# Two moves in a turn-by-turn schedule: the next chunk's key products on Pool, and a read-out's second matmul

## The chip, the cores and the metric

The kernel runs on one core of a Trainium2 chip. Its time is the device time of one execution in microseconds, given as the median of several runs. The engines of the core are named as in the profile: PE does matmuls, PEld is PE's loading of weights, DVE is the vector engine, ACT the scalar engine, POOL the GpSimd engine, and SP only issues DMAs here. Each engine, and SP's queue too, takes its instructions strictly in the order in which they were put.

## The reference, cut to what matters

The program is two layers over x of 16 x 512 x 128 in float32. Layer 0 adds two branches that both read xn, the normalized x: a small memory network that is trained chunk by chunk and then read out (the part that the change touches), and a convolution with attention and a dense mixture of 8 experts. Layer 1 is causal attention done twice and a mixture of 32 experts. The branch in question:

```
x  (16 rows, 512 tokens, 128) -> 8 chunks of 64 tokens
k  = rmsnorm(silu(xc @ wk.T), k_norm_w);   v = silu(xc @ wv.T)
def step((mem, surp), chunk):                   # lax.scan over the 8 chunks, in order
    pred  = k_c + rmsnorm(silu(k_c @ w0.T) @ w1.T, ln)
    grads = grad of mean((v_c - pred)**2 * theta_c) in (w0, w1, ln)
    clip  = min(1 / (norm(grads) + 1e-6), 1)
    surp  = eta_c * surp - grads * clip;  mem = beta_c * mem + surp
q  = rmsnorm(silu(x @ wq.T), q_norm_w)
read-out: q + rmsnorm(silu(q @ w0.T) @ w1.T, ln)     # with the last mem
...
x = x + read-out + attention_and_experts(xn)
```

## The kernel before

The whole program is written as Python generators, "stages", that a small loop (class Turns, L277) advances together. In each turn every live stage runs up to its next `yield` and emits its instructions. Stages carry a rank, and the lower rank goes first within a turn: 0 for the maxima of the attention scores (tops, which calls largest), 1 for the weighted sums (back, which calls weighted), 2 for the ends of those, 3 for the scan and the read-outs, 4 for the rest of attention, 6 for the experts (ffn, L547). PE's order is exactly the order of emission. The other engines and the DMA queues are ordered by the framework, which follows the order of emission as far as its own estimate of readiness lets it; what is marked high priority (rsqrt, L209) is put ahead. A wait therefore stops everything behind it on its engine. The number of expert units that ffn emits in a turn depends on what the other stages put on PE in that turn (`load_ns`), so that turns have about equal PE work.

After a start that normalizes x (norm0), layer 0's attention and experts run in every turn from then to about 1480 us, and beside them one stage, scan (L786). It has two parts.

The chunks. step(c) is one step of the scan. It turns the keys k (turned), makes the hidden layer (hidden, whose last two operations run on Pool, L891 and L892), turns it (hidden_turned), and takes the gradient in two halves (gradient, L901). A half begins with the matmul py, an ACT copy to yh (L914), four squares on ACT with their sums, and Pool's rsqrt giving r_y (L213, L214). Three turns later DVE multiplies yh by r_y (L920), and then a row of DVE products follows (L923 to L942), with one Pool product (gy, L935) between. DVE's maxima of the attention scores (nm, L404) stand between them in the same queue, and each pair of score matmuls needs a PSUM bank that such a maximum sets free. One step takes some 41 turns. On Pool, before() also prepares the decayed state (L853 to L857).

The keys of chunk c + 2 are made by project (L817) beside step(c + 1): it is put on the list at the end of step(c). It loads the tokens, makes four halves of k and v (silu_half, L757), squares k on ACT, calls rsqrt for r_k, and then runs three Pool operations of 128 x 1024 elements, one turn apart: k times the gain (L836), k times r_k (L838), and v = k - v (L840). Two turns later it marks ("keys", c), for which step(c) waits at its beginning. ks and the tiles k and v have two buffers.

The read-outs. After the eighth step, readout(b) (L1024) runs for the 16 rows, started six turns apart, so that about four are alive at a time. Counted from its start: the matmul pj with wq in turn 2, squares and Pool's products for q in turn 4, the transposes into qT in turn 9, the two halves of hidden (L1043: matmul ppq, two ACT operations, a DVE product into hTq) in turns 10 and 11, the sixteen-pass matmul pyq with w1 (L1056 to L1059), the ACT copy yq with four squares and r_yq, three turns later a DVE product (L1065) and three Pool operations (L1066 to L1068), and three turns after that the store to acc (L1070). hTq and yq of row b share a buffer with those of row b + 2 (tags "h" and "ds").

Of the kernel before, what the change touches and what calls it, by code (L numbers as in the profile page):

```python
# [73 lines left out]
def bc(ap, axis, n):  # L74

    u = ap.unsqueeze(axis)
    shape = list(u.shape)
    shape[axis] = n
    return u.to_broadcast(shape)
# [3 lines left out]
def network(ctx: ExitStack, tc: tile.TileContext, a, out):  # L83
# [60 lines left out]
    def mark(*m):  # L144
        done[m] = clock[0]
# [17 lines left out]
    def room():  # L163

        while held[0] >= pools["work"]:
            yield

    def hold(name):

        held[0] += 1  # L170
        return work(name)

    def drop():

        read[0] += 1

    def work(name):
        return pools["ps"].tile([P, 512], F32, tag="bank", bufs=7, name=name)

    def toks(ap):  # L180
        return ap.rearrange("p (t d) -> p t d", d=P)

    def flat(ap):
        return ap.rearrange("p t d -> p (t d)")
# [4 lines left out]
    def mm(o, lhsT, rhs, start=True, stop=True):  # L189
        n = int(np.prod(rhs.shape[1:]))  # L190
        if lhsT.dtype == FR:
            load_ns[0] += 0.5 * (0.45 * n + 105)
        else:
            t = 0.42 * n if lhsT.shape[-1] == 32 and n >= P else 2 * max(0.834 * n, 110)
            load_ns[0] += t
            array_ns[0] += t
        nc.tensor.matmul(o, lhsT=lhsT, rhs=rhs, start=start, stop=stop)  # L197
# [59 lines left out]
    def transpose_tokens(dst, src):  # L257

        nc.scalar.copy(dst, turn4(lambda t: src[:, t, :]))

    def rms_rows(dst, y, n, pool):

        ss = sm.tile([P, n], F32, tag="ss", name="ss")
        for t in range(n):
            sq = pool.tile([P, D], F32, tag="junk", name="sq")
            nc.scalar.activation(sq, y[:, t, :], AF.Square, accum_out=ss[:, t : t + 1])  # L266
        rsqrt(dst, ss, 1.0 / D, 1e-6, n)
# [5 lines left out]
    def idle(n):  # L273
        for _ in range(n):
            yield
# [481 lines left out]
    def silu_half(dst, lhs, w):  # L757

        yield from room()
        p = hold("pj")  # L760
        for t in range(4):
            mm(p[:, t * D : (t + 1) * D], lhs(t), w)
        nc.scalar.activation(dst, p, AF.Tanh)
        yield
        nc.vector.scalar_tensor_tensor(dst, dst, 1.0, p, ALU.add, ALU.mult)
        drop()
        yield

    def side(*parts):

        going, parts = [], list(parts)
        while parts or going:
            if parts:
                going.append(parts.pop(0))
            going = [g for g in going if next(g, StopIteration) is not StopIteration]
            yield
# [9 lines left out]
    def scan(s1):  # L786
# [13 lines left out]
        def tokens_of(c):  # L800
            xc = s1.tile([P, B, CHUNK], F32, tag="gy", name="xc")
            nc.sync.dma_start(xc, xt[0].rearrange("b p (c t) -> c p b t", t=CHUNK)[c])
            return xc.rearrange("p b t -> p (b t)")
# [13 lines left out]
        def project(c):  # L817

            xc = tokens_of(c)
            yield from idle(3)  # L820
            k = s1.tile([P, NT, D], F32, tag="k", bufs=2, name="k")
            v = s1.tile([P, NT, D], F32, tag="v", bufs=2, name="v")

            def half(dst, w, q):
                return silu_half(
                    flat(dst[:, 4 * q : 4 * q + 4, :]),
                    lambda t: xc[:, (4 * q + t) * P : (4 * q + t + 1) * P], A(w),
                )

            yield from side(half(k, "wk", 0), half(k, "wk", 1), half(v, "wv", 0), half(v, "wv", 1))  # L830
            ks[c] = k, v
            mark("read", c)
            rk = sm.tile([P, NT], F32, tag="r_k", name="r_k")
            rms_rows(rk, k, NT, s1)
            yield
            nc.gpsimd.tensor_tensor(k, k, bc(row["kn"], 1, NT), ALU.mult)  # L836
            yield
            nc.gpsimd.tensor_tensor(k, k, bc(rk, 2, D), ALU.mult)  # L838
            yield
            nc.gpsimd.tensor_tensor(v, k, v, ALU.subtract)  # L840
            yield from idle(2)
            mark("keys", c)

        def step(c):
# [138 lines left out]
            if c + 2 < NC:  # L983
                turns.stages.append((turns.turn, 3, project(c + 2)))
# [32 lines left out]
            yield  # L1017

        turns.stages.append((turns.turn, 3, project(0)))
        turns.stages.append((turns.turn + 12, 3, project(1)))  # L1020
        for c in range(NC):
            yield from step(c)

        def readout(b):  # L1024
            xb = s1.tile([P, TB, D], F32, tag=("k", "v")[b % 2], bufs=2, name="xb")
            nc.sync.dma_start(xb, x_b[b])
            xT = s1.tile([P, S], F32, tag=("hT0", "kT")[b % 2], name="xTr")
            nc.sync.dma_start(xT, xt[0, b])
            yield from idle(2)
            q = s1.tile([P, TB, D], F32, tag=("yh", "eb", "gy", "hT1")[b % 4], name="rq")  # L1030
            yield from silu_half(flat(q), lambda t: xT[:, t * P : (t + 1) * P], A("wq"))
            rq = sm.tile([P, TB], F32, tag="r_q", name="r_q")
            rms_rows(rq, q, TB, s1)
            nc.gpsimd.tensor_tensor(q, q, bc(row["qn"], 1, TB), ALU.mult)
            nc.gpsimd.tensor_tensor(q, q, bc(rq, 2, D), ALU.mult)
            yield from idle(5)
            yield from room()
            qT = s1.tile([P, S], F32, tag="sg", bufs=2, name="qT")
            transpose_tokens(qT, q)
            yield from idle(1)  # L1040
            hT = s1.tile([P, 2, S], F32, tag=("h", "ds")[b % 2], name="hTq")

            def hidden(i):  # L1043
                yield from room()
                pp = hold("ppq")
                mm(pp, w0T[:, i * P : (i + 1) * P], qT)
                nc.scalar.activation(hT[:, i, :], pp, AF.Tanh, scale=0.5)
                nc.scalar.activation(hT[:, i, :], hT[:, i, :], AF.Copy, scale=0.5, bias=0.5)
                yield
                nc.vector.tensor_tensor(hT[:, i, :], hT[:, i, :], pp, ALU.mult)  # L1050
                drop()
                yield

            yield from side(hidden(0), hidden(1))
            yield from room()
            py = toks(work("pyq"))  # L1056
            for t in range(TB):
                for i in range(2):
                    mm(py[:, t, :], hT[:, i, t * P : (t + 1) * P], w1T[:, i, :], start=(i == 0), stop=(i == 1))  # L1059
            ry = sm.tile([P, TB], F32, tag="r_yq", name="r_yq")  # L1060
            y = s1.tile([P, TB, D], F32, tag=("h", "ds")[b % 2], name="yq")
            nc.scalar.copy(y, py)
            rms_rows(ry, y, TB, s1)
            yield from idle(3)
            nc.vector.tensor_tensor(y, y, bc(ry, 2, D), ALU.mult)  # L1065
            nc.gpsimd.tensor_tensor(y, y, bc(ln, 1, TB), ALU.mult)  # L1066
            nc.gpsimd.tensor_tensor(y, y, q, ALU.add)
            nc.gpsimd.tensor_tensor(y, y, xb, ALU.add)  # L1068
            yield from idle(3)
            nc.sync.dma_start(acc_b[b], y)  # L1070
            yield
# [3 lines left out]
        while live or b < B:  # L1075
            if b < B:
                live.append(readout(b))
                b += 1
            for _ in range(6):
                live = [g for g in live if next(g, StopIteration) is not StopIteration]  # L1080
                yield
# [572 lines left out]
```

## Time and profile before

| what | value |
|---|---|
| time, median of 3 runs (lowest, highest) | 3565.93 us (3565.69, 3568.84) |
| the profiled execution | 3557.66 us, with a span of 3555.9 us from its first to its last instruction |
| mean granted clock of PE | 0.975 |
| scan's steps | from the first memory update at 249.2 us to the eighth at 1132.0 us |
| read-outs | first ppq at 1163.2 us, last store issued at 1475.3 us |
| L836, L838, L840 on Pool | 8 of each; median 2370, 1898 and 2370 ns |
| L920 on DVE | 16, median 686 ns, longest 1561 ns |
| pyq on PE | 256 passes of 275 ns |

Busy time is the union of an engine's instructions. "Idle before" is the time in which an engine had nothing running before an instruction, and the name behind the arrow is what released it. The profiled execution is one run of its own, 8.3 us below the median of the timed runs, so sums are made against it and then carried to the median.

### The profile page before, as it was taken

The numbers are of one execution on the slowest core, as the hardware profiler recorded it, in microseconds if no ns is written. First come the engines' busy times: TensorE is split into PE (matmuls) and PEld (weight loads), VectorE is DVE, ScalarE is ACT, GpSimd is POOL, SyncE is SP. The second block draws the span as 40 slices with busy tenths as digits, with TensorE's granted clock in tenths as the row PEclk, the third lists the DMA queues.
The fourth block names the chain that finished last, engine by engine and source line by source line (L and its number), as shares of the span: only waits on it lengthen the run. The fifth ranks groups of instructions, "written<-read, shape, count | busy, mean of one in ns | idle before, by whom it ended". The sixth has DMA issues, their size and how long they took to land.

```text
span 3555.9 us, 63951 instructions
## 1 busy us (share of the span) xinstructions
PE 3379.7 (95%) x22085; PEld 1897.3 (53%) x22085; DVE 2315.6 (65%) x6045; ACT 2233.4 (63%) x4951; POOL 1508.2 (42%) x2354
## 2 busy tenths in 40 slices
PE   6999999999999999999999999999999999998887
PEld 3445555554555555455555565555555555554443
DVE  5676666656766566556467667666666666567875
ACT  1566766775766787666656666665666666664444
POOL 5323432432431455432544344443444344433654
PEclk7999999999999999999999999999999999998998
DMA  5222222222122332443434443444344443433343
GB/s 178 70 71 77 71 82 74 74 77 83 56 85 86 102 109 87 133 122 102 135 108 122 124 125 115 130 126 121 107 122 122 124 125 98 134 106 98 93 102 93
DMA packets 289794, 370.37 MB, mean 104 GB/s; under 512 B 45984, under 2 KB 141376, under 8 KB 289088
## 3 DMA queue, kind: packets, MB, share of 16 engines
q1 hardware_dynamic: 282304, 359.46, 35.0%
q0 software_dynamic: 7168, 6.82, 1.2%
q8 instruction: 177, 2.90, 0.3%
q14 instruction: 145, 1.19, 0.1%
HBM read 236.58 MB, written 132.99 MB: 104 GB/s over the span
## 4 chain that ended last, share of the span: by engine, by line
PE 50%; DVE 5%; DMA 3%; ACT 1%; POOL 1%; issue 1%; SPq 1%; POOLq 0%; DVEq 0%; ACTq 0%
PE s L197 13%; PE pye L611 10%; PE phe L197 10%; PE pc L197 9%; PE pq L197 1%; DVE s L396 1%; PE fill L206 1%; DVE nm L404 1%; PE tpc L252 1%; PE tp L252 1%; DVE s L403 1%; PE po L197 1%; ACT e L476 1%; DMA rq<-lo 1%; PE pv L197 1%
## 5 line engine op out<-in xcount | busy, mean ns | idle before, releaser
L476 ACT ACTIVATE e<-s 128x512 f32<-128x512 f32 (+1 forms) x2432 | 1278.3, 577 | 556.4 <-PE s L197 517.2
L404 DVE TENSOR_REDUCE nm<-s 128x1 f32<-128x512 f32 (+2 forms) x1408 | 907.5, 682 | 510.1 <-PE s L197 509.2
L396 DVE CUSTOM_DVE_ANT_0 s<-s,sb_const 128x512 f32<-128x512 f32 (+1 forms) x1024 | 623.4, 643 | 390.3 <-PE s L197 388.9
L484 POOL TENSOR_SCALAR_AFFINE_SELECT e<-e 128x128 f32<-128x128 f32 (+2 forms) x1270 | 429.6, 347 | 751.0 <-ACT e L476 726.5
L197 PE MATMUL s<-kx,qx 64*128 64x512 f32 (+3 forms) x3072 | 620.4, 429 | 26.8 <-DMA kx<-rk 13.5
L197 PE MATMUL pc<-e,vp 128*32 128x512 f32 (+3 forms) x6144 | 621.7, 502 | 13.9 <-POOL e L484 7.8
L611 PEld LDWEIGHTS pye<-ew,hTe 128*128 128x128 f32 x4096 | 519.0, 192 | 178.7 <-issue 157.9
L197 PEld LDWEIGHTS s<-kx,qx 64*128 64x128 f32 x3072 | 271.2, 187 | 555.2 <-issue 219.4
L611 PE MATMUL pye<-ew,hTe 128*128 128x128 f32 x4096 | 562.3, 281 | 1.5 <-ACT hTe L601 1.4
L197 PE MATMUL s<-qx,kx 64*128 64x512 f32 (+3 forms) x3072 | 535.7, 356 | 27.2 <-DVE nm L404 8.4
L197 PE MATMUL phe<-x1T,ew 128*128 128x512 f32 x1024 | 551.1, 623 | 7.8 <-DMA ew<-in_ew 3.1
L601 ACT ACTIVATE hTe<-phe,sb_cols 128x512 f32<-128x512 f32 x512 | 354.1, 692 | 245.2 <-PE phe L197 242.8
L197 PEld LDWEIGHTS s<-qx,kx 64*128 64x128 f32 x3072 | 305.5, 188 | 80.4 <-ACT e L476 19.1
L619 POOL TENSOR_TENSOR ac<-ac,y 128x512 f32<-128x512 f32 x128 | 163.9, 1280 | 425.9 <-ACT y L618 363.9
L403 DVE TENSOR_TENSOR s<-s,sb_const 128x256 f32<-128x256 f32 (+1 forms) x384 | 181.6, 515 | 190.5 <-PE s L197 157.4
L197 PEld LDWEIGHTS pc<-e,vp 128*32 128x32 f32 x6144 | 151.4, 110 | 238.1 <-issue 173.2
L197 PEld LDWEIGHTS phe<-x1T,ew 128*128 128x128 f32 x1024 | 158.8, 193 | 75.0 <-issue 44.1
L618 ACT ACTIVATE y<-pye,pr 128x128 f32<-128x128 f32 x512 | 147.5, 370 | 30.6 <-PE pye L611 26.2
L396 DVE DVE_READ_ACCUMULATOR2_ANT nm<- 128x1 f32 x1024 | 144.1, 141 | 0.0
L213 POOL TENSOR_SCALAR rs_t<-ss 128x4 f32<-128x4 f32 (+1 forms) x56 | 12.0, 215 | 221.5 <-ACT sq L266 220.0
L1470 POOL DMA_INDIRECT acc<-eo,sidx x32 | 52.0, 1624 | 72.2 <-DVE eo L1464 26.3
L213 POOL TENSOR_SCALAR rs_t<-ln_mv 128x4 f32<-128x4 f32 x64 | 12.8, 200 | 162.3 <-DVE ln_mv L223 159.4
(302 smaller groups left out, 3906.4 us busy)
## 6 DMA issues: line engine op xcount, KB each, us to landing
ew<-in_ew SPq DMA_DIRECT2D x256, 256.0 KB
kx<-rk SPq DMA_DIRECT2D x192, 256.0 KB
qx<-rq SPq DMA_DIRECT2D x128, 256.0 KB
rq<-hi SPq DMA_DIRECT2D x64, 256.0 KB
rq<-lo SPq DMA_DIRECT2D x64, 256.0 KB
rk<-hi SPq DMA_DIRECT2D x64, 256.0 KB
rk<-lo SPq DMA_DIRECT2D x64, 256.0 KB
qx<-r SPq DMA_DIRECT2D x64, 256.0 KB
```

What stands on the lines that cost most here:

```text
L197: nc.tensor.matmul(o, lhsT=lhsT, rhs=rhs, start=start, stop=stop)
L252: nc.tensor.transpose(tp[:, t * P : (t + 1) * P], src(t), ident)
L396: newest[0] = nc.vector.tensor_tensor_reduce(out=sv[r][:, 0, :], in0=sv[r][:, 0, :], in1=row["caus"][:, S - n :], scale=1.0, scalar=-BIG, ...
L403: nc.vector.tensor_tensor(dg, dg, bc(row["caus"][:, S - P :], 1, per), ALU.add)
L404: newest[0] = nc.vector.tensor_reduce(nm[:, qt, r, t : t + per], sv[r], AX.X, ALU.max)
L476: nc.scalar.activation(e[:, r, 0 : per * n], s[r], AF.Exp, scale=SCALE)
L484: cleared[0] = nc.gpsimd.affine_select(out=ev[:, r, :, 0:P], in_=ev[:, r, :, 0:P], pattern=[[0, per], [1, P]], compare_op=ALU.is_ge, fill= ...
L601: nc.scalar.activation(hs[i], ph, AF.Relu, bias=col("fb", i))
L611: nc.tensor.matmul(pye[0][:, t, :], lhsT=h[:, t * P : (t + 1) * P], rhs=w2[e][:, f, :], start=(f == 0 and t == 0), stop=(f == 3), skip_gro ...
L618: nc.scalar.mul(y[:, t, :], pye[0][:, t, :], pr[:, t, e : e + 1])
L619: nc.gpsimd.tensor_tensor(ac, ac, y, ALU.add)
L1470: nc.gpsimd.indirect_dma_start(out=acc, out_offset=bass.IndirectOffsetOnAxis(ap=sidx[:, e : e + 1], axis=0), in_=eo[:, i, :], in_offset=No ...
```

## The change

In project, the one `yield` between the rsqrt of the keys and the first long Pool operation becomes nine for the chunks 2 to 7; for chunks 0 and 1 it stays one. L836, L838 and L840, and the mark ("keys", c), are emitted eight turns later. No instruction is added or removed, and project's matmuls, ACT operations and DMAs before this point stay in their turns.

In readout, one turn is put between the hidden halves and the matmul pyq. All that follows in this read-out is emitted one turn later: pyq, yq and its squares, r_yq, L1065 to L1068, and the store to acc.

```
         def project(c):
...
             rms_rows(rk, k, NT, s1)
-            yield
+            yield from idle(9 if c > 1 else 1)
             nc.gpsimd.tensor_tensor(k, k, bc(row["kn"], 1, NT), ALU.mult)
             yield
             nc.gpsimd.tensor_tensor(k, k, bc(rk, 2, D), ALU.mult)
             yield
             nc.gpsimd.tensor_tensor(v, k, v, ALU.subtract)
             yield from idle(2)
             mark("keys", c)
...
         def readout(b):
...
             yield from side(hidden(0), hidden(1))
+            yield from idle(1)
             yield from room()
             py = toks(work("pyq"))
```

`idle(n)` (L273) yields n times.

More of the change, by code (lines that the diff above doesn't have):

```diff
@@ L834, in project @@
             rms_rows(rk, k, NT, s1)
-            yield
+            yield from idle(9 if c > 1 else 1)
             nc.gpsimd.tensor_tensor(k, k, bc(row["kn"], 1, NT), ALU.mult)
@@ L1054, in readout @@
             yield from side(hidden(0), hidden(1))
+            yield from idle(1)
             yield from room()
```

## The prediction

> **What bounds the kernel now.** I read the page's first part, then the busy times by stretch, then the waits of the scan, then the timelines of single engines round one wait.
>
> ```profile
> PE 3379.7 (95%) x22085; PEld 1897.3 (53%) x22085; DVE 2315.6 (65%) x6045; ACT 2233.4 (63%) x4951; POOL 1508.2 (42%) x2354
> ...
> 630.00:760.00 130.00, 126.76 (x750) 71.66 (x751) 86.74 (x162) 88.81 (x201) 47.22 (x46) 0.99 0.25 71
> 760.00:890.00 130.00, 121.56 (x683) 65.99 (x684) 80.44 (x149) 82.19 (x192) 42.20 (x38) 0.96 0.29 88
> 1300.00:1470.00 170.00, 161.43 (x932) 85.13 (x932) 101.89 (x177) 130.84 (x342) 92.52 (x96) 0.97 0.33 100
> ```
>
> PE is the bound, in a fixed order, so only PE's idle time can be won: 130.00 less 126.76 is 3.2 us in one scan step, 8.4 us in the next, and 8.6 us in the second half of the read-outs. Whatever leaves PE waiting anywhere is paid in full, since all later work stands behind it in PE's order.
>
> Next, who waits for Pool. In the waits of 300 to 1160 us (who, for whom, us, times, longest):
>
> ```profile
> DVE yh L920 <- POOL r_y L214: 22.0, 5, 9.9
> PEld s L197 <- DVE nm L404: 31.8, 38, 5.1
> PE s L197 <- DVE nm L404: 13.8, 10, 4.2
> ```
>
> The last two lines are PE waiting for DVE's maxima. The first is DVE standing still for Pool's rsqrt. The timelines of Pool, DVE and PE in step 5 show the link:
>
> ```profile
> 792.88 2.73 POOL L836 TENSOR_TENSOR k<-k,sb_rowsA 128x1024 f32<-128x1024 f32 x1
> 795.55 1.65 POOL L214 TENSOR_TENSOR r_k<-rs_t,nhalf 128x8 f32<-128x8 f32 x1
> 797.28 1.90 POOL L838 TENSOR_TENSOR k<-k,r_k 128x1024 f32<-128x1024 f32 x1
> 799.25 2.34 POOL L840 TENSOR_TENSOR v<-k,v 128x1024 f32<-128x1024 f32 x1
> 801.96 1.01 POOL L214 TENSOR_TENSOR r_y<-rs_t,nhalf 128x4 f32<-128x4 f32 x1
> ...
> 803.00 0.69 DVE L920 TENSOR_TENSOR yh<-yh,r_y 128x512 f32<-128x512 f32 x1 [6.28 <-POOL r_y L214]
> ...
> 804.34 0.79 PE L197 MATMUL s<-kx,qx 64*128 64x512 f32 x2 [4.23 <-DVE nm L404]
> ```
>
> The three key operations stand before r_y of the second gradient half; DVE waits 6.28 us for r_y, the maxima are behind that, and PE stops for 4.23 us.
>
> **Part 1, the keys.** Nothing is added or removed: six times (chunks 2 to 7) 2.37 + 1.90 + 2.37 = 6.64 us of Pool move eight turns. A turn is (1132.0 - 249.2) / 7 / 41 = 3.1 us, so they move 25 us. They start at 270.5, 412.0, 541.1, 651.0, 792.9 and 921.6 us. In the steps of 270.5 and 651.0 they lie well ahead of both halves' r_y; in the other four they lie between the two r_y, and there alone DVE waits at the second half: 9.90, 3.63, 6.28 and 1.18 us.
>
> What goes: without the three, r_y ends 1.4 us after its last square. In the steps of 541, 793 and 922 that is before DVE gets there, so all of the wait goes. In the step of 412 the square ends at 414.25, r_y at 415.6, and DVE has been there since 412.1, so 6.4 of 9.9 go. Sum 6.4 + 3.63 + 6.28 + 1.18 = 17.5 us of DVE. Four DVE products also ran long beside key operations (1561, 1144, 2318 and 1139 ns where 680 is usual), 3.4 us more. Together DVE gets back 20.9 us. PE's gaps put down to DVE's maxima in the 25 us after these four waits are 1.8, 1.7, 4.2 and 3.3 us, 11.0 in all, or 0.53 of PE per us of DVE.
>
> What comes: the three land some 25 us later, at about 295, 437, 566, 676, 818 and 946 us. Pool is idle there (9.3 us before 302.4, 10.8 before 683.0, 10.7 before 447.7, 14.5 before 579.2), so what is queued behind them on Pool is gy (L935), first read by the matmul pln some 20 turns on, an add of the experts, and in one step a layernorm that ends at 830.4 and that PE first reads at 849.7. The mark ("keys") moves to about turn 17 to 21 of a step of 41, still 20 turns ahead of the step that waits for it; were that gone, each turn would cost PE 3.1 us. But here DVE runs the gradient's products, and a product with two SBUF operands that meets a Pool operation is held:
>
> ```profile
> 926.06 1.90 POOL L838 TENSOR_TENSOR k<-k,r_k 128x1024 f32<-128x1024 f32 x1
> ...
> 926.18 2.32 DVE L923 TENSOR_TENSOR gt<-yh,sb_rowsA 128x512 f32<-128x512 f32 x1
> ```
>
> Four of the twelve operations of those steps held a DVE product, by 0.46 to 1.64 us, mean 0.86. Eighteen move (six times three). From below, a third collide as now: 6 x 0.86 = 5.2 us. From above, all at the longest: 18 x 1.64 = 29.5. I take half, since DVE is denser in the gradient than before it but not full: 9 x 0.86 = 7.7 us. Net 20.9 - 7.7 = 13.2 us of DVE, times 0.53: PE gains 7.0 us. Bounds: (20.9 - 5.2) x 0.53 = 8.3 by this ratio and 11.0 if nothing collides; and a loss of (29.5 - 20.9) x 0.53 = 4.6.
>
> The Trainium skill speaks against the move here: "SBUF — State Buffer", section "SBUF: two separate sides", says that a DVE operation with two SBUF inputs and a GpSimd operation take one shared port pair as an exclusive lock for the whole instruction. The pair of rows above agrees: the product started 0.12 us after Pool and ended 0.54 us after it. By the rule alone the worst is every moved Pool operation holding DVE for its whole length, 6 x 6.64 = 39.8 us of DVE, which would turn the gain into an estimated loss of 10 us; the sum above does not use this.
>
> **Part 2, the read-outs.** Sixteen times pyq and all behind it come 3.1 us later. What it can win is one row:
>
> ```profile
> PE pyq L197 <- DVE hTq L1050: 3.0, 1, 3.0
> ```
>
> PE waited for hTq only once, in row 9; elsewhere hTq was ready 1.5 to 6.2 us ahead. So 3.05 us at most, and I take all of it.
>
> Against it, three things. (a) pyq now falls into the turn of the next row's transposes (15 and 9 are equal modulo 6), so ACT has yq's copy and squares ahead of the copy to qT, which ppq needs a turn later. The time from qT's end to ppq is 0.0 to 4.6 us. If qT goes after the copy and one square, as tanh of pj does now, it ends 0.35 us later, and the five rows with less room cost 1.05 us; if after all four squares (0.50 us each), 1.85 us later, 13.2 us over the rows. I take 1.05, the order that the trace shows. (b) The store of row b moves a turn nearer to the first write of hTq of row b + 2. From store to write it is 2.5 us for row 1, where PE then stopped 2.02 us, and 5.9 us or more for all others; one turn comes off that, so one more stall of 3.1 us; I take it. (c) SP's queue waits at this store:
>
> ```profile
> SPq L1070 <- POOL yq L1068: 91.1, 13, 19.0
> ```
>
> Behind the store stand loads for the read-outs, attention and experts. At 1421.63 us the load of x1T went right behind it and PE waited 1.7 us. If it stays behind, 3.1 us more; if it gets in front, 1.7 less; no row decides, so the middle, +0.7. Sum of part 2: -3.05 + 1.05 + 3.1 + 0.7 = +1.8 us, bounds -4.8 and +19.4. The end of the scan hardly moves: the loop over the read-outs goes in groups of six turns, and one more turn fits into the last.
>
> **Sum.** -7.0 + 1.8 = -5.2 us: the profiled execution from 3557.66 to 3552.5, the median from 3565.93 to 3560.7 (the profiled one ran 8.3 us faster, and I carry the difference over).
>
> **The rivals.**
> (B) The wait goes and nothing collides: all 11.0 us and pyq's 3.05, with (a) alone against it: -13.0, 3552.9. For it: only 39 of the gradient's 128 DVE products met a Pool operation of 0.9 us or more at all, and 11 ran long. Against it: the moved operations arrive among just these products.
> (C) DVE's hold takes the place of its wait: all 18 collide at full price, +4.6 + 1.8 = +6.4, 3572.3. For it, the row at 926; against it, the holds of 0.46 us.
> (D) Slower: SP's queue and the shared buffers. Each store one turn later stops what is behind it (loads) or after it (hTq), at 3.1 us a row. With -7.0, -3.05 and +1.05 on the other side it is slower than the bound from six of sixteen rows on; at seven, -9.0 + 21.7 = +12.7, 3578.6. For it: 104 us of SP's waits at this store in 15 of 16 rows. Against it: only two of these reached PE.
> (E) The move does nothing, because the framework orders Pool by readiness and not by emission: 3566. Against it: the keys run as soon as they are emitted.
>
> **How the numbers follow.** Chances: the forecast 0.45, B 0.28, C 0.10, D 0.14, E 0.03. The forecast's own range is 3555 to 3567, and a third of it lies below 3558.8. What a measurement of this kernel can tell from no change is about 0.2%, 7.1 us. Faster: B and a third of the forecast, 0.42. Slower: D and the edge of C, 0.15. Within: the rest, 0.43. The range goes from 3549, where B gets some of the smaller gaps too, to 3572, where C ends; D lies outside.
>
> **What would show it.** Right: the waits of L920 for r_y fall from 23.5 us to about 5, PE's idle time in the four late steps (4.3, 6.9, 8.3, 5.5 us) falls towards the 1.5 to 2.9 of the others, and long products appear among L931 to L942. Wrong: the idle time stays although L920's waits go (C), ppq waits for qT in many rows (a), or loads land late behind acc<-yq (D).

## The result, and the profile after

| kernel | median of the runs | lowest, highest | runs |
|---|---|---|---|
| before | 3565.52 us | 3559.15, 3568.84 | 6 |
| after | 3578.72 us | 3574.25, 3583.32 | 6 |

The ratio is 1.0035, with a 95% interval of 1.0023 to 1.0047: slower, by about 12.5 us, and outside the forecast's range. The profiled execution took 3577.38 us, its span is 3575.6 us, its mean granted clock 0.971 (0.975 before). The page's busy times, and then the busy times by stretch (length; busy time and instructions of PE, PEld, DVE, ACT and POOL; granted clock of PE; DMA share; GB/s), for the stretches shown of before:

```profile
PE 3396.4 (95%) x22085; PEld 1902.6 (53%) x22085; DVE 2319.8 (65%) x6045; ACT 2230.9 (62%) x4951; POOL 1505.2 (42%) x2354
```

```profile
630.00:760.00 130.00, 125.45 (x739) 71.06 (x735) 83.00 (x155) 86.93 (x197) 48.83 (x49) 0.97 0.25 72
760.00:890.00 130.00, 121.67 (x686) 66.03 (x685) 79.07 (x145) 82.89 (x194) 41.39 (x39) 0.96 0.26 80
1300.00:1470.00 170.00, 160.53 (x900) 82.62 (x900) 99.74 (x178) 125.74 (x348) 92.22 (x97) 0.97 0.31 91
```

PE was busy 16.7 us longer with the same 22085 matmuls, and the span grew by 19.7 us. PE's time falls into idle time, time lost to half clock (half of its busy time under a granted clock of 0.5), and the rest, its own work at full clock:

| | before | after | difference |
|---|---|---|---|
| idle | 176.2 | 179.2 | +3.0 us |
| lost to half clock | 70.6 | 79.6 | +9.0 us |
| own work at full clock | 3309.1 | 3316.8 | +7.7 us |

The second row lies within what executions of one order differ by: e1 below, with the order of before on every queue, lost 80.9 us to half clock in its profile.

By stage, the scan up to its last memory update grew from 1132.0 to 1137.8 us with the same 1.5 to 8.3 us of idle time in every step: only half clock grew (20.7 to 28.1 us). From the first to the last ppq it took 291.0 us and now 294.3. A later stretch in layer 1, between the attention's passes at 2150 and 2263 us of before, grew from 112.4 to 121.9 us: 2.8 us more idle time, 3.3 us of half clock and 3.3 us more of PE's own work. Its rows, cut at whole microseconds near these points, in before and then in after:

```profile
2150.00:2263.00 113.00, 112.15 (x838) 66.41 (x837) 77.52 (x239) 74.88 (x158) 51.72 (x111) 1.00 0.44 129
```

```profile
2163.00:2285.00 122.00, 118.36 (x850) 69.76 (x849) 78.39 (x239) 75.93 (x162) 53.16 (x112) 0.97 0.41 119
```

The read-outs' 3.3 us and this stretch's 9.5 us are 12.8 us, by one profile each, against 13.2 us between the medians; the scan's 5.8 us are half clock.

The waits of 300 to 1160 us hold the forecast's main line unchanged (who, for whom, us, times, longest):

```profile
DVE yh L920 <- POOL r_y L214: 22.0, 5, 9.9
```

This should have fallen to about 5. The timelines of Pool and DVE in step 5 (start, us, engine, line, operation, tiles) show why it did not:

```profile
798.49 2.73 POOL L836 TENSOR_TENSOR k<-k,sb_rowsA 128x1024 f32<-128x1024 f32 x1
...
802.89 1.90 POOL L838 TENSOR_TENSOR k<-k,r_k 128x1024 f32<-128x1024 f32 x1
804.86 2.34 POOL L840 TENSOR_TENSOR v<-k,v 128x1024 f32<-128x1024 f32 x1
...
807.57 1.01 POOL L214 TENSOR_TENSOR r_y<-rs_t,nhalf 128x4 f32<-128x4 f32 x1
...
808.61 0.69 DVE L920 TENSOR_TENSOR yh<-yh,r_y 128x512 f32<-128x512 f32 x1 [6.28 <-POOL r_y L214]
```

The keys' three operations stand before r_y exactly as they did (before, L836 started at 792.88 and L920 had the same 6.28 us). They did not move.

In the read-outs the wait of pyq for hTq is gone, and another has come, of s for hTq. That of ppq for qT is not new: it was 0.9 us in before. The waits of PE and of ACT from 1160 to 1490 us:

```profile
PE s L197 <- DVE hTq L1050: 5.7, 2, 5.2
...
PE ppq L197 <- ACT qT L259: 0.8, 1, 0.8
```

```profile
ACT hTq L1047 <- DMA acc<-yq: 6.2, 2, 5.4
```

ACT waits for a DMA, the store of a read-out, before it writes hTq. The 5.4 us are in row 8. The timelines there:

```profile
1310.91 3.14 POOL L237 TENSOR_SCALAR x<-x,ln_mv,ln_rs 128x128 f32<-128x128 f32 x4
...
1315.48 1.27 POOL L245 TENSOR_TENSOR x<-x,sb_rows 128x512 f32<-128x512 f32 x1
1316.71 1.28 POOL L619 TENSOR_TENSOR ac<-ac,y 128x512 f32<-128x512 f32 x1
1317.94 1.28 POOL L1067 TENSOR_TENSOR yq<-yq,sb_rowsA 128x512 f32<-128x512 f32 x1
...
1320.65 1.27 POOL L1069 TENSOR_TENSOR yq<-yq,xb 128x512 f32<-128x512 f32 x1
...
1321.94 0.37 SPq L1071 DMA_DIRECT2D acc<-yq  x1
...
1324.48 0.60 ACT L1047 ACTIVATE hTq<-ppq 128x512 f32<-128x512 f32 x1 [5.41 <-DMA acc<-yq]
...
1325.97 0.69 DVE L1050 TENSOR_TENSOR hTq<-hTq,ppq 128x512 f32<-128x512 f32 x1 [5.83 <-ACT hTq L1048]
...
1326.72 0.79 PE L197 MATMUL s<-qx,kx 64*128 64x512 f32 x2 [5.17 <-DVE hTq L1050]
1327.44 2.07 PE L611 MATMUL pye<-ew,hTe 128*128 128x128 f32 x8
```

Read it upwards from PE: 5.17 us idle for DVE's product, which waited for ACT, which waited for the store of row 6, because hTq of row 8 lies in the buffer of yq of row 6. The store was late because yq's three Pool operations came after the attention's layernorm (L237 to L245) and an add. In before the three ran ahead of that layernorm and the store was issued at 1307.05. Counted from the first ppq of each kernel (1163.2 and 1169.0 us), the store went from 143.9 to 152.9 us: 9 us later, not one turn. The last line shows what came on top: eight passes of pye took 2.07 us, where a group of eight takes 1.16 us at full clock.

### The profile page after: what moved, and what is told of

Read it like the earlier page. It is cut to its first block, busy times and chain, and to the rows that moved or that the text cites. A ratio compares the mean times of both kernels' runs of the same rounds, so it can differ in the third digit from the quotient of the medians.

```text
span 3575.6 us, 63951 instructions
## 1 busy us (share of the span) xinstructions
PE 3396.4 (95%) x22085; PEld 1902.6 (53%) x22085; DVE 2319.8 (65%) x6045; ACT 2230.9 (62%) x4951; POOL 1505.2 (42%) x2354
## 5 line engine op out<-in xcount | busy, mean ns | idle before, releaser
L197 PE MATMUL s<-qx,kx 64*128 64x512 f32 (+3 forms) x3072 | 544.3, 357 | 43.0 <-DVE nm L404 9.1
L618 ACT ACTIVATE y<-pye,pr 128x128 f32<-128x128 f32 x512 | 147.7, 370 | 34.5 <-PE pye L611 29.8
L396 DVE DVE_READ_ACCUMULATOR2_ANT nm<- 128x1 f32 x1024 | 143.9, 141 | 0.0
L213 POOL TENSOR_SCALAR rs_t<-ln_mv 128x4 f32<-128x4 f32 x64 | 12.8, 200 | 175.3 <-DVE ln_mv L223 172.6
```

The lines of the kernel that those rows point to most:

```text
L396: newest[0] = nc.vector.tensor_tensor_reduce(out=sv[r][:, 0, :], in0=sv[r][:, 0, :], in1=row["caus"][:, S - n :], scale=1.0, scalar=-BIG, ...
L618: nc.scalar.mul(y[:, t, :], pye[0][:, t, :], pr[:, t, e : e + 1])
```

## The experiments

None of the kernels leaves out a part of the reference. Ratios are to the kernel before, measured beside it on the same chip, with 95% intervals:

| experiment | median | ratio | interval |
|---|---|---|---|
| e1, part 1 alone | 3567.98 | 1.0002 | 0.999 to 1.0015 |
| e2, pyq a turn later, experts' turns kept | 3569.66 | 1.0013 | 1.0 to 1.0027 |
| e3, experts' new turns alone | 3564.30 | 0.9993 | 0.998 to 1.0005 |
| e4, only what follows yq's squares a turn later | 3577.24 | 1.0027 | 1.0014 to 1.0041 |
| e5, after, with an own buffer for yq | 3559.23 | 0.999 | 0.9981 to 1.0 |
| e6, e4 with the own buffer | 3548.49 | 0.995 | 0.9937 to 0.9963 |
| e7, before with the own buffer | 3554.47 | 0.9969 | 0.9957 to 0.998 |
| e8, the keys really behind r_y | 3558.74 | 0.9987 | 0.9978 to 0.9995 |
| e9, e6 once more | 3562.51 | 0.996 | 0.9945 to 0.9974 |
| e10, e2 with the own buffer | 3567.06 | 0.9981 | 0.9968 to 0.9995 |
| e11, e9 with the keys of four chunks behind r_y | 3555.60 | 0.9947 | 0.9931 to 0.9962 |
| e12, e9 with the keys behind gy | 3573.47 | 0.9991 | 0.9978 to 1.0004 |

The medians of before in the three groups were 3564.86 (e1 to e4), 3563.46 (e5 to e8) and 3573.73 us (e9 to e12), so the ratios are to be compared, not the medians.

### Part 1 alone (e1)

```
-            yield
+            yield from idle(9 if c > 1 else 1)
```

> Part 1 of the change alone on the kernel before. Theory N (the framework puts Pool's key operations where its own estimate has them ready, whatever the turn of their emission): Pool's order, the key operations at 412, 541, 793 and 922 us and DVE's waits for r_y (9.9, 3.6, 6.3, 1.2 us) stay, ratio 1.000 within 0.002. Rival M (the part moves something and takes a share in the loss): waits of L920 other than these, ratio 1.001 to 1.004. This run also serves as a measure of what two executions of one order differ by in time and granted clock.

No change: 1.0002. The order of the instructions on each of the five queues, with what they wait for, is that of before from the first to the last. The framework put the three operations where its estimate of readiness had them, whatever turn they were emitted in. Part 1 changes nothing in the program's order, and everything that after lost comes from part 2.

### Part 2 taken apart (e2, e3, e4)

Part 2 does three things: pyq comes a turn later, the experts' units (which fill the turns by `load_ns`) fall into other turns, and the tail, all from L1065 to the store, comes a turn later. e2 moves pyq but books its load in the old turn, so that PE's order is before's except for pyq's place; the tail moves with it:

```
+            load_ns[0] += 1760.0
+            array_ns[0] += 1760.0
+            yield from idle(1)
+            load_ns[0] -= 1760.0
+            array_ns[0] -= 1760.0
             yield from room()
             py = toks(work("pyq"))
```

> Part 2 alone, pyq one turn later with all behind it, but its PE load is still booked in the old turn, so that the experts' units keep the turns of the kernel before; PE's order differs in pyq's place alone. Theory P (the loss comes from the experts' units that are planned anew, to the end of the experts in layer 1): ratio 0.999 to 1.001, about 3563 to 3567 us. Rival R (the loss lies in the read-outs: hTq, the squares ahead of qT, the later store): ratio 1.003 to 1.004, about 3578 us.

1.0013: between the ranges of the two theories. Its profile has the stop of row 8 that after has (ACT 6.19 us at hTq, then PE 4.71 us), but 112.4 us in the stretch at 2150 us. e3 leaves pyq in its turn and books its load in the next one:

```
+            load_ns[0] -= 1760.0
+            array_ns[0] -= 1760.0
...
-            yield from idle(3)
+            yield from idle(1)
+            load_ns[0] += 1760.0
+            array_ns[0] += 1760.0
+            yield from idle(2)
```

> The kernel before with pyq in its old turn, but its PE load booked one turn later, so that the experts' units take the turns of the kernel after and no read-out moves. Theory P: ratio 1.003 to 1.004, about 3578 us. Rival R: 0.999 to 1.001.

0.9993, no difference in the time, as rival R had it. Its profile holds two opposite ones: from the first to the last ppq it took 283.4 us (291.0 before), and in the stretch at 2150 us 119.1 us (112.4 before). That stretch took 112.4 to 112.7 us in each of the eleven profiles without the experts' new turns, and 119.1, 121.9 and 122.1 us in the three with them (e3, after, e5): its growth comes from these turns. PE's own work at full clock is 3315.5 us in e3, 3316.8 in after and 3315.7 in e5, the three kernels with the experts' new turns; in the other eleven profiles it lies between 3304 and 3311. The score matmuls with qx as the first operand hold most of the difference (336.0 us in before, 343.6 in e3, 344.4 in after).

e4 moves the tail alone, with PE's order that of before:

```
-            yield from idle(3)
+            yield from idle(4)
             nc.vector.tensor_tensor(y, y, bc(ry, 2, D), ALU.mult)
```

> pyq in its old turn; only what is behind yq's squares (DVE's product, Pool's three, the store) one turn later. PE's order is that of the kernel before. Theory P: ratio 0.999 to 1.001. Rival S (SP's queue stands longer behind the later stores, and hTq behind its buffer): ratio 1.002 to 1.004, with loads landing late behind the store and PE gaps before ppq or pyq of 3 us each.

1.0027: the tail alone is slower. The timelines of SP and ACT in row 8:

```profile
1317.09 0.37 SPq L1070 DMA_DIRECT2D acc<-yq  x1
...
1319.66 0.60 ACT L1047 ACTIVATE hTq<-ppq 128x512 f32<-128x512 f32 x1 [4.29 <-DMA acc<-yq]
```

ACT stands 4.29 us, until 2.6 us after the issue of the store, and PE then has a gap of 3.3 us before ppq, which before has not. A gap of 3.05 us before pyq follows 28 us later, but that one stands in before too. From the first to the last ppq e4 took 298.1 us (291.0 before).

### The shared buffer taken away (e5, e6, e7, e9, e10)

hTq and yq of a row get parts of one tile, and the next row but one no longer writes hTq into what yq is being stored from; SBUF is the same for the rest:

```
+        both = [s1.tile([P, 4 * S], F32, tag=("h", "ds")[i], name="hTyq") for i in range(2)]
...
-            hT = s1.tile([P, 2, S], F32, tag=("h", "ds")[b % 2], name="hTq")
+            hT = both[b % 2][:, 0 : 2 * S].rearrange("p (i s) -> p i s", i=2)
...
-            y = s1.tile([P, TB, D], F32, tag=("h", "ds")[b % 2], name="yq")
+            y = toks(both[b % 2][:, 2 * S : 3 * S])
```

> The kernel after, with yq beside hTq in its buffer and not over it, so that hTq of row b + 2 no longer waits for the store of row b; PE's order is that of the kernel after. Theory B (the loss is ACT standing at hTq for the late store, 5.4 us, and the half clock that follows PE's gap): no such wait of ACT, the gap of 5.2 us before PE's s at 1327 us gone with the half clock behind it, ratio about 1.001 (what the experts' new turns cost in layer 1 stays). Rival P (all of the loss is the experts' turns) or Q (SP's queue behind the later store): the ratio stays at 1.003 to 1.004.

> The kernel with the tail alone one turn later (1.0027 before), with yq beside hTq. Theory B: 0.998 to 1.000. Rival Q (SP's queue): stays at 1.002 to 1.003.

> The kernel before with yq beside hTq. Theory B: the gaps of 2.0 us before ppq of row 3 and 3.05 us before pyq of row 9 go, with the half clock behind the second (1.7 us): some 6 us, ratio 0.998 to 0.999. Rival P: 1.000.

PE's order and SP's order stay as they were in each pair. ACT's and DVE's do not: without the shared buffer the framework puts some of hTq's operations earlier (56 places differ on ACT between after and e5, 18 on DVE), so the own buffer is a wait less and some order besides.

In after the ratio fell from 1.0035 to 0.999. The timelines of e5 in row 8 (Pool, SP, ACT; hTq and yq are now called hTyq):

```profile
1305.30 3.13 POOL L237 TENSOR_SCALAR x<-x,ln_mv,ln_rs 128x128 f32<-128x128 f32 x4
...
1309.86 1.27 POOL L245 TENSOR_TENSOR x<-x,sb_rows 128x512 f32<-128x512 f32 x1
...
1315.04 1.28 POOL L1071 TENSOR_TENSOR hTyq<-hTyq,xb 128x512 f32<-128x512 f32 x1
...
1316.35 0.37 SPq L1073 DMA_DIRECT2D acc<-hTyq  x1
...
1313.38 0.61 ACT L1049 ACTIVATE hTyq<-ppq 128x512 f32<-128x512 f32 x1
```

The layernorm still runs ahead of yq's operations and the store is still late, but ACT writes hTq of row 8 at 1313.38, 2.97 us before the store of row 6 is even issued. With the shared buffer it would have stood until some 2.5 us after the issue, 5.5 us: the 5.41 of after. The busy times from 1300 to 1350 us, in e5 and then in after:

```profile
1300.00:1350.00 50.00, 49.76 (x291) 25.84 (x291) 29.37 (x49) 39.14 (x104) 34.59 (x35) 1.00 0.40 111
```

```profile
1300.00:1350.00 50.00, 44.76 (x257) 23.17 (x257) 27.42 (x49) 35.03 (x104) 28.44 (x32) 0.93 0.26 78
```

5.0 us of PE and the lost clock are back. From the first to the last ppq e5 took 283.2 us against 294.3, of which 6.7 were idle time and 4.3 half clock. e4 became e6: from 1.0027 to 0.995, though the store of row 6 still comes 148.0 us after the first ppq (143.9 in before, 151.0 in e4). SP's queue has the same stores in the same order in e6, so no loss that can be measured is left for it: what cost was the write behind the store, not what stands behind the store in the queue. In e7 before's gaps of 2.0 and 3.05 us are gone. e6 and e7 came out faster than theory B had them. The own buffer is worth something in every pair: 0.31% in before, 0.45% in after, 0.77% in e4 (0.67% by e9, the same kernel again).

> The kernel of e6 once more, as the base for the two behind it on this chip: 0.994 to 0.997 if its 0.995 holds; 0.997 to 0.998 if it was no better than the kernel before with the same buffers (e7).

> Part 2 with its PE load booked in the old turn (1.0013 before), with yq beside hTq: against e5 it differs in the experts' turns alone, against e9 in pyq's turn alone. If the experts' new turns cost the difference between e5 and e6 (0.4%): 0.995 to 0.997. If pyq's own later turn costs it: 0.998 to 1.000.

e9 is the kernel of e6 again, 0.996 after 0.995. e10 against e2 gives 0.32% for the buffer once more. e10 and e9 differ in pyq's turn alone (with yq's copy and squares behind it), 0.9981 against 0.996 with intervals that overlap: that pyq's later turn costs anything is likely, not shown.

### The keys really moved (e8, e11, e12)

To test what part 1 meant to do, the first key operation is tied to come after r_y's product tr (L921) of the second half:

```
+            yield from idle(9 if c > 1 else 1)
+            with ExitStack() as behind:
+                if c > 1:
+                    yield from after(("half", c - 1))
+                    behind.enter_context(tc.issue_after(halves[c - 1].ins))
...
-                nc.gpsimd.tensor_tensor(tr[:, a4], ry[:, a4], th[:, a4, c], ALU.mult)
+                halves[c] = nc.gpsimd.tensor_tensor(tr[:, a4], ry[:, a4], th[:, a4, c], ALU.mult)
+                if q == 1:
+                    mark("half", c)
```

> The kernel before, with Pool's key operations of chunks 2 to 7 tied behind the gradient's second r_y, as part 1 was meant to do; only Pool's order differs. Theory K (the prediction's part 1): DVE's waits for r_y fall from 23.5 us to about 5, PE idle in the four late steps falls from 25 to some 14 us, a product or two runs long in each step beside the key operations: -7 us and the half clocks behind the gaps, ratio 0.997 to 0.998. Rival L (DVE's products are held by the key operations as long as they had waited): ratio 0.999 to 1.001, with the long products among L923 to L942.

0.9987, a gain that the interval just separates from none, between the ranges of the two theories. In the four late steps the tie moved the first key operation 4 to 5 us, counted from the step's memory update, and 22 us in the other two: behind r_y, but not as far as the forecast's 25 us. The waits for r_y fell from 23.5 to 6.3 us, as the forecast had it, but PE's idle time in the six steps did not: 29.8 us before, 30.5 now. The timelines of Pool and DVE in step 6 show where it went:

```profile
930.01 2.37 POOL L840 TENSOR_TENSOR k<-k,sb_rowsA 128x1024 f32<-128x1024 f32 x1
...
934.02 2.34 POOL L842 TENSOR_TENSOR k<-k,r_k 128x1024 f32<-128x1024 f32 x1
936.44 2.69 POOL L844 TENSOR_TENSOR v<-k,v 128x1024 f32<-128x1024 f32 x1
...
931.48 1.44 DVE L931 TENSOR_TENSOR gt<-gt,v 128x512 f32<-128x512 f32 x1
...
935.73 1.18 DVE L937 TENSOR_TENSOR gy<-gt,yh 128x512 f32<-128x512 f32 x1
936.84 2.84 DVE L929 TENSOR_TENSOR gt<-yh,sb_rowsA 128x512 f32<-128x512 f32 x1
```

L929 needs 0.68 us alone; here it ends 0.55 us after the Pool operation that it met. Fifteen products were held beside the eighteen moved operations, by 19.5 us in all (four and 3.4 us before): DVE got 17.2 us of waiting back and gave 16.1 us more in holds. This is the rival in which the hold takes the place of the wait. The row of L929 agrees with the rule in the Trainium skill, "SBUF — State Buffer", section "SBUF: two separate sides", which the prediction weighed: the lock lasts for the whole instruction of the other engine.

e11 is e9 with the tie for chunks 3, 4, 6 and 7 alone, those whose operations lay between the two r_y:

```
+            yield from idle(9 if c in (3, 4, 6, 7) else 1)
+            with ExitStack() as behind:
+                if c in (3, 4, 6, 7):
```

> e9 with Pool's key operations tied behind the second r_y in the four steps with a wait alone (chunks 3, 4, 6, 7). Theory L (DVE's products held by the key operations give back most): 0 to 2 us below e9. Theory K: 5 us or more below e9, since the two steps that e8 made longer by 4.8 and 3.2 us stay as they were.

0.9947, the lowest median beside e9, e10 and e12, 6.9 us under e9's. By the median that is theory K's line and not theory L's, but the intervals overlap, so it is not shown that the keys add to the buffer's gain. PE's idle time in the six steps is 28.5 us against e9's 30.0; ten products were held, by 12.8 us. Up to the first ppq its profile is 9.5 us shorter than e9's, and 8.6 us of that are half clock, which differs between executions of one order too. e12 ties the keys of chunks 2 to 7 behind the second half's gy (L935), where fewer gradient products are left:

```
+                halves[c] = nc.gpsimd.tensor_tensor(gy, gy, bc(th[:, a4, c], 2, D), ALU.mult)
```

> e9 with the key operations of chunks 2 to 7 tied behind the gradient's second gy on Pool, past all but the last products of the gradient. If what gives the gain back in e8 is the hold of DVE's products (theory L), this place has fewer of them: at most six products above 0.8 us beside key operations (15 in e8), the waits for r_y near 5 us, PE idle in steps 1 to 6 near 20 us (30.5 in e8), 5 to 8 us below e9. If the hold is not the cause: no more than 2 us below e9.

This missed: 11 us slower than e9. In the four late steps the first key operation came 18 to 22 us later in its step than in before, near the forecast's place, and more was held there, not less: twelve products, by 15.5 us, and eight small operations of DVE, by 13.3 us, together 28.8 us (20.3 in e8, where one small operation was held). PE's idle time in the six steps rose to 36.1 us. The timelines of Pool, DVE and PE in step 1:

```profile
312.21 2.22 POOL L842 TENSOR_TENSOR k<-k,r_k 128x1024 f32<-128x1024 f32 x1
314.52 2.67 POOL L844 TENSOR_TENSOR v<-k,v 128x1024 f32<-128x1024 f32 x1
...
310.41 2.27 DVE L947 TENSOR_TENSOR gt<-yh,m 128x512 f32<-128x512 f32 x1
...
313.20 1.78 DVE L948 TENSOR_TENSOR gt<-gt 128x512 f32<-128x512 f32 x1
314.91 2.31 DVE L943 TENSOR_SCALAR m<-m 128x4 f32<-128x4 f32 x1
...
318.65 0.45 PE L418 MATMUL tpm<-sb_const,mp 128*128 128x128 f32 x1 [5.11 <-DVE mp L411]
```

Behind the held operations stood DVE's maxima, one of which PE needs for tpm; it stopped for 5.11 us. So the premise failed, that this place has fewer holds; the loss itself is what the hold, theory L's cause, would bring.

## Why the prediction was wrong, step by step

**PE is the bound, in a fixed order, and idle time is paid in full.** Right, but not the whole price. After a stop PE also runs at half clock for a while, which no term of the sum had: the 5.17 us of row 8 cost another 2.6 us (half of its work from 1326.72 to 1332.0 us).

**Part 1, -7.0 us.** The step that failed is its first: "they move 25 us". They moved on no queue (e1), and the sum was over nothing; rival E, to which 0.03 was given, is what happened to part 1. "The keys run as soon as they are emitted" stood on one trace; Pool's order is set by the framework, and a trace of one order can't tell emission and readiness apart. e8 and e12 test the rest of the chain. The wait that goes was sized well (17.2 us against 17.5). The hold was not: 7.7 us were forecast, nine operations at 0.86; e8 held 19.5 us, fifteen products at 1.30, and e12, whose places are nearer to the forecast's, 28.8 us. The upper bound of 29.5 us had held both; taking half was the error. 0.53 of PE per us of DVE could not show in e8, since DVE's net came to about nothing; in e12 DVE lost more than it got back and PE's idle time rose by 6.1 us over e9's.

**Part 2, +1.8 us.** The -3.05 for pyq came: its wait is gone. (a), ppq behind qT, was forecast at 1.05 and cost nothing that shows: PE's waits for qT are 0.8 us in after and were 0.9 in before. (c), SP's queue, forecast at +0.7, was not seen to cost anything: the 1.7 us that PE waited for x1T in before are not there in after (nor in e3, so the move of pyq need not be the reason). (b) is the term that was mis-sized: the right mechanism, the store of row b and the write of hTq in row b + 2, but one stall of 3.1 us was taken, in the row after row 1, and 5.9 us or more of room for "all others" was called safe. Row 8 had 6.2 us of room and was the one that stopped, for 5.2 us of PE and 2.6 of half clock; the 2.0 us of the row after row 1 went. The step took "a turn later" to be 3.1 us; on Pool the three operations lost their place to a layernorm and an add, and the store came 9 us later.

And no term stood for the experts' units, which fall into other turns when pyq's load does. That is the larger omission: 9.5 us in the stretch at 2150 us, long after the last read-out. e2, with the same stop in row 8 and the old turns, measured 1.0013 where after measured 1.0035. In e3, where they alone move, the read-outs were 7.6 us shorter with the same turns, and the time stayed; in after the stop of row 8 took that gain away.

**The rivals.** D's 3578.6 us lies at the measured 3578.72, but for another reason: D had SP's queue and seven rows at 3.1 us; it was one row at 7.8 us and the experts' turns in layer 1. That nearness is no proof of D.

**What stays open.** e5 against e7, 0.999 and 0.9969, is what after still loses with the buffer out of the way, some 7.5 us. The profiles put it in the stretch at 2150 us, 122.1 us in e5 and 112.4 in e7, with the read-outs 1.1 us shorter in e5. Why the experts' new turns cost there, no run takes apart. pyq's later turn may add to it; the ratios of e3, e5 and e10 don't add up well enough to divide the loss to a tenth of a per cent. And 5.8 us of the profiled difference lie before the read-outs, where the order is the same and only the half clock differs: that part is one execution's and not the change's.

## What to carry to other kernels

Before costing a moved emission, find out who orders the queue that it goes to; where it is a framework's estimate of readiness, a `yield` is no order, and only a tie is. A buffer that a store reads from and that the next stage writes into couples that stage's engine to everything ahead of the store; its slack is counted against the longest operations that can slip in front of it, not against a turn. Where a planner fills turns by load, moving one item plans everything behind it anew, and that has to be priced to the end of the plan. Trading a wait of an engine for holds on the same engine won nothing here, since what is queued behind is what PE needs.

## What the runs showed of the hardware

A stop of PE is followed by half clock more often, and after shorter stops, than the prediction reckoned with. The granted clock behind row 8's stop in after, in stretches of 2 us:

```profile
1327.00:1329.00 2.00, 2.00 (x9) 1.57 (x9) 1.46 (x3) 2.00 (x8) 0.33 (x2) 0.50 0.22 54
1329.00:1331.00 2.00, 2.00 (x5) 0.64 (x4) 0.69 (x1) 0.99 (x3) 2.00 (x2) 0.50 0.21 78
1331.00:1333.00 2.00, 2.00 (x12) 1.32 (x12) 1.02 (x2) 1.40 (x3) 2.00 (x3) 0.75 0.25 81
1333.00:1335.00 2.00, 2.00 (x14) 0.83 (x16) 0.60 (x2) 1.06 (x2) 1.92 (x3) 1.00 0.81 259
```

The clock is at half until 1332.0 us, 6.8 us in all from 1325.2, so from 3.6 us after PE had stopped. In the fourteen profiles of this case, from 200 to 1480 us, 36 of 37 gaps over 2.5 us had a half-clock stretch of 3.4 us or a multiple beginning by 4 us after the gap's end, and 44 of 132 gaps of 1.0 to 2.5 us (many are the same place in kernels of nearly one order); it began 1.5 to 4.8 us after the start of the long gaps and cost 2.4 us beside the gap on the mean. The Trainium skill, "TensorE: Matmul & The Clock Gate", section "HAM oscillation — how this bites in real kernels", gives idle gaps over about 3.4 us as what to avoid. All fourteen gaps above that length had half clock behind them here, but so had 22 of the 23 from 2.5 to 3.4 us and a third of those from 1.0 to 2.5 us; a plan for this kernel had better count 2 to 3 us more for each stop of PE over 2.5 us.

The same stretches come and go between executions of one order (70.6 us lost in before's profile, 80.9 in e1's): before took between 3556.50 and 3578.18 us over 35 runs, the three fastest at a mean granted clock of 0.973 to 0.974 and the three slowest at 0.968 to 0.969. That spread is wider than the 13.2 us between the medians of before and after.

A small operation is held as well as a large one: L943 works on 128x4 values with one input tensor and took 2.31 us beside a Pool operation, where it takes 0.15 to 0.17 us alone.
